# Two-layer graph attention with residual layernorms: the sums of x1 emitted right behind its transposes, and the opening's exponentials and weight sums in other places

## The chip, the core and the metric

The kernel runs on one core of a Trainium2 chip, as one launch. The metric is device time in microseconds (us); the median of three runs is taken. Times in the profile count from the first instruction of one profiled execution.

## The reference

The input x holds 128 graphs of 64 nodes with 768 features, so 8192 tokens; `adj` is a 64x64 mask for each graph. Two layers follow one another, each `layernorm(x + gnn(x))`, all in fp32.

Layer 0 is a gated graph attention with 12 heads of 64 features:

```
h    = x @ W                           # per head
attn = src(tanh(h)) + dst(tanh(h))^T   # src, dst: dot products with w_src, w_dst
attn = leaky_relu(attn, 0.2); attn = where(adj, attn, -999); p = softmax(attn)
f    = elu(p @ h + b);  gate = sigmoid(x @ H_w.T + H_b)
x1   = layernorm(x + gate * f + (1 - gate) * x)
```

Layer 1 is dense attention with 6 heads of 128 features inside each graph:

```
q, k, v = x1 @ Wq, x1 @ Wk, x1 @ Wv
out = layernorm(x1 + softmax(q k^T / sqrt(128), masked) v @ Wf + bf)
```

## The kernel before, in words

**Tiles.** A tile is 128 tokens (two graphs), a pair `p` is two tiles, `t0 = 2p` and `t1 = 2p + 1`. There are 32 pairs. The first half of the span (to about 1490 us) does layer 0 for every pair and the product for `v` of layer 1. The second half does q, k, attention and the output of layer 1; the change does not touch it.

**Products.** A 256x768x768 product is done by a Strassen scheme on 2x2 blocks: seven block products of three matmuls each, instead of eight. Class `Job` holds one such product: "h" (x @ W), "g" (the gate) and "v" (x1 @ Wv). Block product number i of job h is written h1 to h7. Products 3, 5, 6 and 7 need sums of the input's blocks, s4, s1, s2 and s3 (`block_sums`, L240 to L243); products 4 to 7 read sums of weight blocks (`weight_sums`, L216 to L219; product 4 reads T4, 5 reads T1, 6 reads T2, 7 reads T3, made at L218, L216, L217 and L219). For h and g the input sums are `sx`, made by GpSimd (POOL) from x. For v they are `sv`, made by VectorE (DVE) from `x1T`, the transposed x1.

Several products of a job accumulate in the same bank of PSUM: y takes 1, 6, 7, 4 one on top of the other, and between them the partial sum has to be read out ("way out": `S.copy` on ScalarE, ACT, for h and v; an addition on DVE for the gate). So h6 waits for the way out of h1, h7 for that of h6, h4 for that of h7.

**Order.** Everything is emitted in the order of the program, and each engine works through its own list in that order. A turn of the loop over `p` runs a list of products (FIRST for p = 0, SECOND for p = 1, then TURN); after product number `pos` of the list, the previous product's way out is emitted, then the other steps that have been put at `pos`. The steps belong to the new pair p (`at(pos, new, ...)`) or to the old pair q = p - 1 (`was(pos, ...)`); the tables FIRST_AT, SECOND_AT, SECOND_OLD, THIRD_AT and LAST_AT shift a position in the first, second, third and last turn. A position past the end of a list is carried into the next turn: with 13 products in FIRST, position 16 of turn 0 is position 3 of turn 1.

**Steps of a tile.** `products` (tanh of h on ACT, a multiplication on DVE, L889, and one on POOL, L890), `terms` (a reduction to `sd` on DVE, L897, a store to DRAM, `dstd`, and two loads that spread it, `dd`), `with_bias` (POOL, L913, and two loads `hx`), `logits` (DVE, L926, needs dd), `leaky` (ACT, L936), `masked` (three DVE operations, L942 to L949), `exps` (ACT, L955, writes `prob`). In the next turn: `probs_by_nodes` (TensorE, PE, transposes prob into PSUM bank `pTp`, ACT copies it to `pT`), `attend` (PE, `av`), `features` (DVE reads av, L1003 and L1004; ACT exp, L1011), `gate_tanh` (ACT, L1067 and L1068), `residual` (POOL, L1017), `elu1`, `gated`, `stats`, `normed` (layernorm: DVE, POOL, ACT), `by_features` (PE transposes x1 into `x1Tp`, ACT copies it to `x1T`), then `v_begins`, which sets up the sums `v_sums` and the job v, the four sums, and `spill_features`, a store of x1T. SyncE (SP) issues all transfers from one list.

In the regular turn `by_features(t0)` stands at 11, `v_begins` at 12, `products(n0)` at 12, `terms(n1)` at 13, v1 and v2 are products 14 and 15, g4 is 16, v6, the first to need a sum of x1 (s2), is 17.

During turns 2 to 30 POOL also makes sums of the weights for the second half (`sum_weights`, L366).

Of the kernel before, what the change touches and what calls it, by code (L numbers as in the profile page):

```python
# [52 lines left out]

FIRST = ["h1", "h2", "h5", "h6", "g1", "h7", "g2", "h4", "g6", "g5", "g7", "h3", "g3"]

FIRST_AT = {3: 0, 6: 10, 8: 3, 11: 8, 12: 12, 13: 12, 14: 13, 15: 14, 16: 14, 17: 14, 18: 15, 19: 16, 20: 17}
SECOND = [
    "h1", "G4", "h2", "g1", "g2", "h6", "h5", "h7", "g6", "h4",
    "g5", "g7", "h3", "g4", "g3", "H1", "v1", "v2", "v6", "v5", "v7", "H2",
]  # L60
SECOND_AT = {11: 10, 12: 13, 13: 13, 14: 14, 15: 14, 16: 15, 17: 16, 18: 18, 19: 19, 20: 20}
SECOND_OLD = {
    7.5: 12, 0: 7, 1: 7, 2: 8, 3: 9, 4: 10, 5: 11, 6: 12, 7: 12, 8: 13, 9: 14, 11: 15, 12: 15, 15: 16, 16: 17, 19: 19,
}


# [29 lines left out]
    + [f"q{n}" for n in (0, 1, 2, 3, 4, 5, 6, 8, 7, 9, 10, 11, 12)]  # L96
    + ["v1", "v2", "v6", "q13", "v5", "v7", "q14", "v4", "v3"]
)
LAST_AT = {7.5: 8, 3: 3, 4: 4, 5: 5, 6: 6, 7: 7, 8: 9, 9: 10, 11: 12, 12: 13, 15: 15, 16: 17, 19: 18}


PARTS = ("v", "sp", "sc", "ex", "mult", "split", "send", "turn", "join", "cp", "ctx")
# [24 lines left out]
TURNS = {  # L127
    0: (FIRST, FIRST_AT, {}),
    1: (SECOND, SECOND_AT, SECOND_OLD),
# [5 lines left out]
def kernel(  # L135
# [34 lines left out]
    V, S, G, T = nc.vector, nc.scalar, nc.gpsimd, nc.tensor  # L170
# [30 lines left out]
    def load_weight(src, tag, name, order=(B11, B21, B22, T3)):  # L201

        w = wpool.tile([P, 7, HK, HALF], F32, tag=tag, name=name)
        for block in order:
            load_block(src, w, block)
        return w
# [6 lines left out]
    def weight_sums(eng, w):  # L213

        return [
            lambda: eng.tensor_tensor(w[:, T1], w[:, T3], w[:, B11], ALU.subtract),  # L216
            lambda: eng.tensor_tensor(w[:, T2], w[:, B22], w[:, T1], ALU.subtract),  # L217
            lambda: eng.tensor_tensor(w[:, T4], w[:, B21], w[:, T2], ALU.subtract),  # L218
            lambda: eng.tensor_tensor(w[:, T3], w[:, B22], w[:, T3], ALU.subtract),  # L219
        ]  # L220
# [535 lines left out]
    with ExitStack() as ph, ExitStack() as ph_r:  # L756
# [43 lines left out]
        hw_w = weights["k"] = load_weight(hwT, "wb", "hw_wk", (B11, B21, T3, B22))  # L800
# [5 lines left out]
        t1, t2, t4, t3 = weight_sums(V, w0_w)  # L806
        all_of((t1, t2, t3, t4))
        wv_w = wpool.tile([P, 7, HK, HALF], F32, tag="wc", name="wv")
# [30 lines left out]
        def h_job(p):  # L839
            def at(m, n):  # L840
                return h_of(p, m)[:, n * J0 : (n + 1) * J0, :E0]

            def as_heads(b):
                return b.rearrange("p (j e) -> p j e", e=E0)

            return token_job(
                f"h{p}",
                A[p],
                w0_w,
                lambda mn, b: S.copy(at(*mn), as_heads(b)),  # L850
                lambda mn, b: V.tensor_tensor(at(*mn), as_heads(b), at(*mn), ALU.add),
                lambda b: S.copy(at(1, 0), as_heads(b)),
            )

        def gate_job(p):
            def at(m, n):
                return gate_of(p, m)[:, n * HALF : (n + 1) * HALF]

            def bias(n):
                return hb_bc[:, n * HALF : (n + 1) * HALF]  # L860

            return token_job(
                f"g{p}",
                A[p],
                hw_w,
                lambda mn, b: V.tensor_tensor(at(*mn), b, bias(mn[1]), ALU.add),
                lambda mn, b: V.tensor_tensor(at(*mn), b, at(*mn), ALU.add),
                lambda b: V.tensor_tensor(at(1, 0), b, bias(0), ALU.add),
            )
# [213 lines left out]
        def value_sums(q):  # L1083
            B[q], v_sums[q] = sums_of(V, sb, "sv", x1Ts[q], f"v{q}")
# [21 lines left out]
        v_sums, carried = {}, {}  # L1106
        summing = sum_weights(sb)
        for p in range(NP + 1):
            q = p - 1
            new, old = p < NP, 0 <= q < NP  # L1110
            t0, t1, n0, n1 = 2 * q, 2 * q + 1, 2 * p, 2 * p + 1
            if new:
                jobs["G"] = jobs.get("g")
                jobs["h"], jobs["g"] = jobs["H"] if p == 2 else h_job(p), gate_job(p)
            plan = {}

            turn, of_new, of_old = TURNS.get(p, (TURN, {}, {})) if new else (LAST, {}, LAST_AT)

            def at(pos, ok, *acts, places=of_new):
                if ok:  # L1120
                    plan.setdefault(places.get(pos, int(pos)), []).extend(acts)

            def was(pos, *acts):
                at(pos, old, *acts, places=of_old)

            def do(f, *args):
                return lambda: f(*args)

            def v_begins():
                value_sums(q)  # L1130
                jobs["v"] = v_job(q)


            was(0, do(probs_by_nodes, t1))
            at(0, old, do(exps, t0), do(gate_tanh, t1), places={0: 6} if p == 1 else of_old)
            was(1, do(residual, t1))
            was(2, do(attend, t1), do(gate_tanh, t0))
            was(3, do(features, t1), do(probs_by_nodes, t0), do(residual, t0))
            was(4, do(elu1, t1), do(gated, t1))
            was(5, do(attend, t0), do(stats, t1))  # L1140
            was(6, do(features, t0), do(normed, t1))
            was(7, do(elu1, t0))
            was(7.5, do(gated, t0))
            was(8, do(by_features, t1), do(stats, t0))
            was(9, do(normed, t0))
            was(12, do(v_begins))
            was(15, lambda: v_sums[q][0](), lambda: v_sums[q][1](), do(spill_features, q))
            was(16, lambda: v_sums[q][2]())
            was(19, lambda: v_sums[q][3]())

            at(0, p + 1 < NP, do(load_xT, p + 1))
            at(3, new, lambda: adjs.__setitem__(p, load_adj(sb, 2 * p, PAIR, f"adj_{p}")))
            at(6, new, do(mask, p))
            at(4, 0 <= p - 2 < NP, do(spill_values, p - 2))
            at(8, new, do(inputs, p))
            at(11, new, do(products, n1))
            was(11, do(by_features, t0))
            at(12, new, do(products, n0))
            at(13, new, do(terms, n1), do(with_bias, n1))
            at(14, new, do(terms, n0), do(with_bias, n0))  # L1160
            at(15, new, do(plus_one, p))
            at(16, new, do(logits, n1))
            at(17, new, do(leaky, n1))
            at(17, p + 1 < NP, do(x_sums, p + 1), places={17: 12} if p == 0 else of_new)
            at(18, new, do(masked, n1), do(logits, n0))
            at(19, new, do(exps, n1), do(leaky, n0))
            at(20, new, do(masked, n0))

            if p == NP - 1:

                at(2, True, do(load_wide, "q", wq, range(4)))
                at(8, True, do(load_wide, "q", wq, range(4, 8)))
                at(12, True, do(load_wide, "q", wq, range(8, NW)))
                at(9, True, do(load_wide, "k", wk, range(4)))
                at(15, True, do(load_wide, "k", wk, range(4, 8)))
                at(18, True, queries_begin)
                at(20, True, do(load_wide, "k", wk, range(8, NW)), lambda: jobs["rows"].ready(2))
            if p == NP:
                flush()
                for act in plan.pop(0):  # L1180
                    act()
            if p == 0:
                for pos, act in zip((6, 7, 8, 9), weight_sums(V, hw_w)):
                    at(pos, True, act, places={})
                for block in (B11, B21, T3, B22):
                    at(8, True, do(load_block, wv, wv_w, block))
                at(7, True, lambda: V.tensor_scalar(b01_bc, b01_bc, 1.0, None, ALU.add))
            if p == 1:
                at(14, True, third_begins, places={})
                for pos, act in zip((4, 5, 7, 8), weight_sums(V, wv_w)):  # L1190
                    at(pos, True, act, places={})
            for pos, acts in carried.items():
                plan[pos] = acts + plan.get(pos, [])
            carried = {pos - len(turn): acts for pos, acts in plan.items() if pos >= len(turn)}
            for pos, item in enumerate(turn):
                step(jobs[item[0]], int(item[1:]))
                for act in plan.get(pos, ()):
                    act()
                if 2 <= p < NP - 1:
                    for _ in range(1 + pos % 2):  # L1200
                        next(summing, None)
                if item[0] == "q":
                    jobs["rows"].ready(int(item[1:]) + 4)
            if p == NP - 2:
                drain(summing)
            if old:
                jobs["u"] = jobs["v"]
# [4 lines left out]
    with ExitStack() as ph:  # L1212
# [45 lines left out]
        for g in range(1, NG):  # L1258
# [26 lines left out]
            p = 2 * g - 2  # L1285
# [7 lines left out]
        p = 2 * NG - 2  # L1293
# [66 lines left out]
```

## Time and profile before

| | |
|---|---|
| median of 3 runs | 2900.05 us (2900.02 to 2900.45) |
| the profiled execution, whole | 2898.46 us |
| its span, first to last instruction | 2896.7 us |
| PE busy | 2844.1 us (98%) |
| DVE busy | 1936.7 us (67%) |
| POOL busy | 1289.3 us (45%) |
| ACT busy | 1061.6 us (37%) |
| mean granted PE clock | 0.997 |

The table says how long each engine was busy in the span. A line of the timeline gives the start, the duration, the engine, the source line, the operation, what it writes and reads, the shapes, how many instructions were merged, and in square brackets how long the engine was idle before it and what it waited for. A block product of three matmuls counts six there[...].

### The profile page before, as it was taken

The page shows a single profiled execution, that of the slowest core. Times are in us where ns is not written, and L with a number is a line of the kernel's source. Part 1 is how long each engine was busy: PE and PEld are TensorE (multiplying, and loading weights), DVE is VectorE, ACT ScalarE, POOL GpSimd, SP SyncE. Part 2 cuts the span into 40 slices and gives each one's busy share as a digit, 9 for nine tenths or more (in the row PEclk, how much of TensorE's full clock was granted, in tenths as well). Part 3 has the DMA queues.
Part 4 walks back from the last instruction along what each step waited for, and adds up shares of the span by engine and source line. Part 5 has one row for each costly group of instructions (what it writes and reads, how often), then busy time and mean ns, then how long its engine had stood idle before and what let it go on. Part 6 is the DMA issues. An engine that isn't in the chain of part 4 may idle for free.

```text
span 2896.7 us, 47873 instructions
## 1 busy us (share of the span) xinstructions
PE 2844.1 (98%) x18252; PEld 2074.9 (72%) x18252; DVE 1936.7 (67%) x3203; ACT 1061.6 (37%) x1896; POOL 1289.3 (45%) x1253
## 2 busy tenths in 40 slices
PE   7899999999999999999999999999999999999998
PEld 4566556665566655666668888888888888888886
DVE  6888788888878888887874545555545555554556
ACT  2444444444444444444443123333213333322332
POOL 2434454444535444333443454444545443444534
PEclk9999999999999999999999999999999999999999
DMA  5344444544444444333353434432324333223332
GB/s 176 116 154 154 149 136 150 159 142 149 144 154 147 141 141 139 120 122 104 119 203 83 124 101 110 107 91 75 86 82 111 110 101 93 70 84 95 110 88 74
DMA packets 322068, 348.73 MB, mean 120 GB/s; under 512 B 147888, under 2 KB 247216, under 8 KB 321840
## 3 DMA queue, kind: packets, MB, share of 16 engines
q1 hardware_dynamic: 321840, 345.66, 39.1%
q8 instruction: 146, 2.39, 0.4%
q14 instruction: 82, 0.67, 0.1%
HBM read 198.48 MB, written 122.29 MB: 111 GB/s over the span
## 4 chain that ended last, share of the span: by engine, by line
PE 84%; DVE 8%; DMA 3%; ACT 2%; issue 1%; POOL 1%; SPq 1%; POOLq 0%; DVEq 0%; ACTq 0%
PE z_o L494 8%; PE z_k L447 8%; PE z_q L447 8%; PE y_h L270 7%; PE y_v L270 6%; PE y_g L270 6%; PE y_k L447 6%; PE y_o L494 6%; PE y_q L447 5%; PE z_h L270 4%; PE z_v L270 3%; PE z_g L270 3%; PE x_g L270 2%; PE sp L550 2%; PE cp L634 2%; PE x_h L270 2%
## 5 line engine op out<-in xcount | busy, mean ns | idle before, releaser
L574 ACT ACTIVATE sc<-sc 128x512 f32<-128x512 f32 x48 | 30.7, 639 | 615.0 <-DVE sc L571 615.0
L695 POOL TENSOR_TENSOR y<-y,bf_bc 128x768 f32<-128x768 f32 x64 | 114.7, 1815 | 288.3 <-DMA y<-x1d 288.3
L507 DVE TENSOR_TENSOR y<-y,z_o 128x256 f32<-128x256 f32 x320 | 127.5, 418 | 139.6 <-PE z_o L494 139.4
L494 PE MATMUL z_o<-wf,so 128*128 128x256 f32 x896 | 215.8, 383 | 2.3 <-DVE y L507 1.2
L447 PE MATMUL z_q<-xs,w_wq 128*128 128x256 f32 x896 | 213.5, 381 | 0.3 <-POOL xs L411 0.3
L411 POOL TENSOR_TENSOR so<-ctxT 128x256 f32<-128x256 f32 x224 | 160.1, 731 | 92.3 <-PE y_o L494 47.0
L447 PE MATMUL z_k<-xs,hw_wk 128*128 128x256 f32 x840 | 198.5, 379 | 0.0
L1017 POOL TENSOR_TENSOR x<-gate,x 128x768 f32<-128x768 f32 x64 | 118.2, 1848 | 159.6 <-ACT gate L1068 145.3
L494 PEld LDWEIGHTS z_o<-wf,so 128*128 128x128 f32 x896 | 167.2, 190 | 26.9 <-issue 2.0
L447 PEld LDWEIGHTS z_q<-xs,w_wq 128*128 128x128 f32 x896 | 168.7, 190 | 24.3 <-POOL xs L411 0.7
L322 POOL TENSOR_TENSOR rs_b<-ve_b,minus_half 128x1 f32<-128x1 f32 x64 | 40.5, 632 | 312.9 <-DVE ve_b L320 312.1
L890 POOL TENSOR_TENSOR th<-th,wsd 128x768 f32<-128x768 f32 x64 | 117.3, 1832 | 139.8 <-DVE th L889 139.8
L447 PEld LDWEIGHTS z_k<-xs,hw_wk 128*128 128x128 f32 x840 | 159.5, 190 | 21.7
L322 POOL TENSOR_TENSOR rs_a<-ve_a,minus_half 128x1 f32<-128x1 f32 x64 | 36.0, 562 | 307.8 <-DVE ve_a L320 307.8
L411 POOL TENSOR_TENSOR xs<-r,r 128x512 f32<-128x512 f32 x112 | 147.7, 1336 | 39.3 <-DMA r<-x1Td 22.1
L462 DVE TENSOR_TENSOR qT<-qT,z_q 128x512 f32<-128x512 f32 x96 | 66.0, 688 | 141.7 <-PE z_q L447 141.7
L270 PE MATMUL y_v<-wv,sv_v 128*128 128x384 f32 x384 | 136.4, 491 | 9.3 <-DVE sv_v L241 7.5
L270 PE MATMUL y_h<-w_wq,xT 128*128 128x384 f32 x384 | 136.5, 492 | 8.7 <-DMA w_wq<-in_w_dram 8.1
L462 DVE TENSOR_TENSOR kT<-kT,z_k 128x512 f32<-128x512 f32 x96 | 66.1, 688 | 112.3 <-PE z_k L447 111.2
L270 PE MATMUL y_h<-w_wq,sx_x 128*128 128x384 f32 x384 | 136.5, 492 | 4.2 <-ACT h L850 4.2
L270 PE MATMUL y_g<-hw_wk,sx_x 128*128 128x384 f32 x384 | 136.2, 491 | 2.5 <-DVE hw_wk L219 2.2
L270 PE MATMUL z_v<-wv,sv_v 128*128 128x384 f32 x384 | 137.5, 494 | 1.0 <-DVE v L880 1.0
(165 smaller groups left out, 6913.3 us busy)
## 6 DMA issues: line engine op xcount, KB each, us to landing
x<-in_x_dram SPq DMA_DIRECT2D x64, 384.0 KB, 3.6
dd<-dstd SPq DMA_DIRECT2D x128, 192.0 KB, 3.4
x1d<-x SPq DMA_DIRECT2D x64, 384.0 KB, 2.6
x1Td<-x1T SPq DMA_DIRECT2D x32, 768.0 KB, 4.3
vd<-v SPq DMA_DIRECT2D x64, 384.0 KB, 3.1
r<-x1Td SPq DMA_DIRECT2D x96, 256.0 KB, 3.5
v<-vd SPq DMA_DIRECT2D x384, 64.0 KB, 2.3
y<-x1d SPq DMA_DIRECT2D x64, 384.0 KB, 5.4
```

What stands on the lines that cost most here:

```text
L270: T.matmul(to[:, : self.n], lhsT, rhs, start=kc == 0 and not more, stop=kc == HK - 1, skip_group_check=more,)
L322: G.tensor_tensor(rstd, ve, minus_half, ALU.pow)
L411: G.tensor_tensor(t, self.of(x[0]), self.of(x[2]), x[1])
L447: T.matmul(b[:, half * W2 : (half + 1) * W2], w[:, kc, half * P : (half + 1) * P], x[:, kc, :], start=half == kc == 0 and not more, stop=k ...
L462: V.tensor_tensor(at, at, b.rearrange("p (h t) -> p h t", h=2), ALU.add if sign > 0 else ALU.subtract,)
L494: T.matmul(b[:, :W2], x[:, kc, :], w[:, kc, :], start=kc == 0 and not more, stop=kc == 1, skip_group_check=more,)
L507: V.tensor_tensor(at, at, self.banks[path][:, :W2], ALU.add if sign > 0 else ALU.subtract)
L550: T.matmul(self.sp_[gr * N : (gr + 1) * N, (i * 2 + a) * N : (i * 2 + a + 1) * N], qT[:, 2 * self.f + a, at], kT[:, 2 * self.f + a, at], s ...
L634: T.matmul(self.cp_[a][e, at], self.v_[rows, i, gr, e], self.scT_[rows, at], start=True, stop=True,)
L695: G.tensor_tensor(y, y, pools["bf"], ALU.add)
L890: G.tensor_tensor(th[:, 1, :], th[:, 1, :], wsd[:, 1, :], ALU.mult)
L1017: G.tensor_tensor(xp, st[t]["gate"], xp, ALU.mult)
```

## The change

It moves instructions and adds none.

1. `v_begins` now stands after `by_features(t0)` in the text, and emits the first sum of x1 (s1) with it at position 12; the second (s2) goes to 13. Both stood at 15. SECOND_OLD and LAST_AT get an entry for 13. `spill_features` stays at 15, the sums s3 and s4 at 16 and 19.
2. In turn 0, the weight sums of the gate: T3 is emitted at 8 and T4 at 9, where T4 was at 8 and T3 at 9.
3. In turn 1, the weight sums of v: T1, T2 and T4 all at 0, where they stood at 4, 5 and 7. T3 stays at 8.
4. For pair 0: `exps(1)`, `leaky(0)` and `masked(0)` from positions 3, 3 and 4 of turn 1 to 6; `exps(0)` and `gate_tanh(1)` from 6 to 8; `residual(1)` from 7 to 8.

```diff
-FIRST_AT = {3: 0, 6: 10, 8: 3, 11: 8, 12: 12, 13: 12, 14: 13, 15: 14, 16: 14, 17: 14, 18: 15, 19: 16, 20: 17}
+FIRST_AT = {3: 0, 6: 10, 8: 3, 11: 8, 12: 12, 13: 12, 14: 13, 15: 14, 16: 14, 17: 14, 18: 15, 19: 19, 20: 19}
 SECOND_OLD = {
-    7.5: 12, 0: 7, 1: 7, 2: 8, 3: 9, 4: 10, 5: 11, 6: 12, 7: 12, 8: 13, 9: 14, 11: 15, 12: 15, 15: 16, 16: 17, 19: 19,
+    7.5: 12, 0: 7, 1: 8, 2: 8, 3: 9, 4: 10, 5: 11, 6: 12, 7: 12, 8: 13, 9: 14, 11: 15, 12: 15, 13: 15, 15: 16, 16: 17, 19: 19,
 }
-LAST_AT = {7.5: 8, 3: 3, 4: 4, 5: 5, 6: 6, 7: 7, 8: 9, 9: 10, 11: 12, 12: 13, 15: 15, 16: 17, 19: 18}
+LAST_AT = {7.5: 8, 3: 3, 4: 4, 5: 5, 6: 6, 7: 7, 8: 9, 9: 10, 11: 12, 12: 13, 13: 14, 15: 15, 16: 17, 19: 18}
...
-            at(0, old, do(exps, t0), do(gate_tanh, t1), places={0: 6} if p == 1 else of_old)
+            at(0, old, do(exps, t0), do(gate_tanh, t1), places={0: 8} if p == 1 else of_old)
...
-            was(12, do(v_begins))
-            was(15, lambda: v_sums[q][0](), lambda: v_sums[q][1](), do(spill_features, q))
+            was(15, do(spill_features, q))
...
             was(11, do(by_features, t0))
+
+            was(12, do(v_begins), lambda: v_sums[q][0]())
+            was(13, lambda: v_sums[q][1]())
             at(12, new, do(products, n0))
...
             if p == 0:
-                for pos, act in zip((6, 7, 8, 9), weight_sums(V, hw_w)):
+                h1, h2, h4, h3 = weight_sums(V, hw_w)
+                for pos, act in zip((6, 7, 8, 9), (h1, h2, h3, h4)):
                     at(pos, True, act, places={})
...
             if p == 1:
                 at(14, True, third_begins, places={})
-                for pos, act in zip((4, 5, 7, 8), weight_sums(V, wv_w)):
+                for pos, act in zip((0, 0, 0, 8), weight_sums(V, wv_w)):
                     at(pos, True, act, places={})
```

Compared engine by engine, the lists of PE and SP are the same in both programs. The list of DVE differs in every turn of the first half; those of ACT and POOL differ in turn 1 alone.

## The prediction

> **What bounds the kernel now.** I read the page first, then PE's waits, then the timelines of the opening and of one regular turn. PE is busy for nearly the whole span, and the change neither adds nor reorders a PE instruction, so only PE's waits, and the slow matmuls behind them, can move the time.
>
> ```profile
> PE 2844.1 (98%) x18252; PEld 2074.9 (72%) x18252; DVE 1936.7 (67%) x3203; ACT 1061.6 (37%) x1896; POOL 1289.3 (45%) x1253
> ```
>
> PE's waits, by who ended them:
>
> ```profile
> PE y_h L270 <- DMA w_wq<-in_w_dram: 8.1, 1, 8.1
> PE y_v L270 <- DVE sv_v L241: 7.5, 9, 1.4
> PE y_h L270 <- ACT h L850: 4.8, 2, 4.2
> PE x1Tp L966 <- ACT x L327: 4.5, 2, 3.3
> ...
> PE y_g L270 <- DVE hw_wk L219: 2.2, 1, 2.2
> ```
>
> The first is the load at the start and stays. The second is v6 waiting for s2, in nine turns (0.62 us in turn 1, 6.9 in later ones, 7.0 with a wait of 0.12 too short for the list). The rest lies in turns 0 and 1. PE's timeline there, g7, h3 and g3 of pair 0, then h5 and h7 of pair 1:
>
> ```profile
> 33.03 3.39 PE L270 MATMUL y_g<-hw_wk,sx_x 128*128 128x384 f32 x6 [2.16 <-DVE hw_wk L219]
> 36.22 2.65 PE L270 MATMUL z_h<-w_wq,sx_x 128*128 128x384 f32 x6
> 38.70 2.10 PE L270 MATMUL z_g<-hw_wk,sx_x 128*128 128x384 f32 x6
> ...
> 52.24 2.10 PE L270 MATMUL z_h<-w_wq,sx_x 128*128 128x384 f32 x6
> 58.52 4.18 PE L270 MATMUL y_h<-w_wq,sx_x 128*128 128x384 f32 x6 [4.18 <-ACT h L850]
> ```
>
> A product costs 2.10 us, and 1.94 from start to start; behind a wait over 2 us it is slower. DVE in the same stretch, T4 and T3 of the gate, the second reduction to sd and the first logits:
>
> ```profile
> 28.74 1.35 DVE L218 TENSOR_TENSOR hw_wk<-hw_wk 128x1152 f32<-128x1152 f32 x1
> ...
> 30.48 2.50 DVE L219 TENSOR_TENSOR hw_wk<-hw_wk 128x1152 f32<-128x1152 f32 x1
> ...
> 43.37 1.75 DVE L897 TENSOR_REDUCE sd<-th 128x24 f32<-128x1536 f32 x1
> 48.99 2.75 DVE L926 TENSOR_TENSOR att<-dd,sd 128x768 f32<-128x768 f32 x1 [3.88 <-DMA dd<-dstd]
> ```
>
> g7 waits for L219. DVE then sits 3.88 us for dd, and from 48.99 on it is almost never idle until features(1) at 71.49. A regular turn on DVE:
>
> ```profile
> 1236.28 0.55 DVE L851 TENSOR_TENSOR h<-z_h,h 128x384 f32<-128x384 f32 x1
> 1237.91 1.17 DVE L889 TENSOR_TENSOR th<-th,wsd 128x768 f32<-128x768 f32 x1 [1.08 <-ACT th L888]
> 1239.00 1.74 DVE L897 TENSOR_REDUCE sd<-th 128x24 f32<-128x1536 f32 x1
> ...
> 1243.37 1.31 DVE L240 TENSOR_TENSOR sv_v<-x1T 128x384 f32<-128x384 f32 x1
> 1244.71 1.23 DVE L241 TENSOR_TENSOR sv_v<-sv_v,x1T 128x384 f32<-128x384 f32 x1
> ```
>
> s1 and s2 come after two reductions, though x1T was complete at 1237.13 (ACT's copies).
>
> **What the Trainium skill says.** "SBUF — State Buffer", "Who interferes with whom": a VectorE tensor_tensor with both inputs in SBUF and a GpSimd operation that reads SBUF lock each other out for a whole instruction; tensor_reduce never contends. The trace agrees: L926 took 2.75 us while POOL ran L913, 1.50 without; L897 took 1.75 beside a POOL multiplication. "TensorE: Matmul & The Clock Gate", "Part 1: The HAM clock gate", says that activity releases a throttle on PE's clock. The trace agrees in kind: behind 2.16 us of waiting the product took 3.39 us, behind 1.4 us 2.17.
>
> **Part 2, T3 ahead of T4.** T3 takes T4's slot at 28.74 and ends at 30.1; PE wants g7 at 30.87. The wait of 2.16 goes, and with it the slow stretch: g7 to h3 takes 3.19, h3 to g3 2.48, against 1.94 each, so 1.79. Together 3.95 us. T4 now runs until 33.0 and is wanted by G4 at about 38.5. One addition (L866) stands between the two in both orders.
>
> **Part 3, three weight sums of v.** 3 x 1.27 us (start to start) leave DVE's full stretch after 49 and fill its wait for dd. Their blocks had landed by 34.25 and the sums come after both reductions, so dd isn't delayed. But POOL then runs L890, L913, the four sx and L913, 41.4 to 50.4. In alternation each sum waits for a POOL operation of about 1.0. With everything 4.0 earlier, the reductions end at 41.1; the sums run 41.8-43.1, 44.05-45.3, 46.3-47.6, with sx in between; logits(1) starts behind the fourth sx, 48.6 to 50.1. Shifted alone it would have been 45 to 47.7. So the fight costs 2.4 of the 4.0. POOL's sx come in time: s2 at 44.05 for h6 at 46.2, s3 at 46.3 for h7 at 50.
>
> **Part 4, exponentials.** Now h7 waits 4.18 since the way out of h6 stands on ACT behind exps(1) and leaky(0). It moves ahead of both, and only leaky(1) remains in front, to 51.0. So h7 starts at 51.5 (PE ready at 50.05), not 54.5. Next late is prob(1): masked(1) ends at 54.05 on DVE, exps(1) at 54.95, so the transposes wait until 55.0 (ready 53.4). g6 waits for the addition L866 until 56.55. Attend follows at 58.5, and through POOL's memset the way out of h7, at 60.1; exps(0), which now stands behind it, ends at 60.95, when its input is ready anyway. features(1) ends at 63.8 (before 71.49, 7.7 earlier). gate_tanh(0) and residual(0) follow late: POOL's L1017 (1.82) then locks out elu1 at 64.5 to 66.3, which costs 1.3. The tile's x1 comes at 69.1 instead of 75.45: 6.4 us earlier. This chain (DVE, ACT, layernorm) ends PE's waits before the x1 transposes, so PE gains the same. No transfer is reissued elsewhere: SP's list is unchanged, and its stores simply come earlier.
>
> The opening thus gives 6.4, plus 0.6 as s2 now stands ahead of the logits, 7.0. Without the fight for the port, logits(1) is 3.7 earlier and the sum is about 11. Were Part 4 to bring nothing, Part 2 alone gives 4.0.
>
> **Part 1, s1 and s2.** Regular turn: s1 may start at 1237.2, in the idle time before L889, but POOL's L890 (1236.44 to 1238.26) locks it out; it ends at 1238.8. L889 ends at 1239.7 (before 1239.08), s2 at 1240.2. v6 wants s2 at 1246: its wait goes in every turn, 7.0 us. Behind s1 and s2 now queue both reductions. The first ends at 1241.9 instead of 1240.74: dstd, dd and logits come 1.2 later. In this turn dd landed at 1246.43 and was read at 1247.14, so logits lose 0.5. exps(1) ended at 1254.30, and PE's transposes began 1.55 later: hidden, with 1.05 left. The gate's additions (L866) slip 1.2, to 1242.4, and g4 reads them at 1244.14. In turns with L366 on POOL the delay may be 2.0, and a turn whose 1.4 us wait goes has that much less slack: in the turn at 693 us I find 0.86 slack against 0.7 to 1.4 of delay. I take 1.0 off for such turns: 6.0 of 7.0 kept (bounds 3.0 and 7.5). In turn 31 dd comes late (4.63 idle) behind weight loads that land until 1473, so the 1.2 mostly disappears there; 0.2 lost, at most 1.2.
>
> **Sum.** -7.0 -6.0 +0.2 = -12.8 us. The profiled execution took 2898.46 (span 2896.7 and 1.76 around it) and becomes 2885.7; it ran 1.6 below the median of 2900.05. Taken off the median: 2887.2 us.
>
> **Rivals.**
> (a) The opening without the fight: -11.4 -6.5, 2882. For it: PE and POOL drift, and nothing forces alternation. Against: POOL is busy throughout, and L926 did take 2.75 there.
> (b) Half the gain: the later dd hands back 3 to 4 us in the turns that waited, and the opening gives only Part 2's 4.0 and a little: -5 to -9, 2891 to 2894.5. For it: the slack of 0.86 above.
> (c) No difference: the opening's wait for one late thing is replaced by the next, as PE is early to everything there, and the turns hand back theirs; under 5.8 us. Against: Part 2 has no cover, its 4.0 alone almost reach the bound.
> (d) Slower: dd. Logits have 0.55 to 1.5 us between landing and reading, then 1.55 to the transposes, so about 2.1 in each turn. A delay of 2.8 would cost 0.7 in each of 30 turns, 21 us, and the sum becomes +7: 2907. It decides from 2.5 on (12 us, gain gone). For it: POOL operations of 1.82 and 0.74 can hit s1 and s2 both. Against: where they fell thickest I find 2.0, and much of a delay is idle time in front of L889 already.
>
> **How the numbers follow.** Main case 0.60 (2883.5 to 2891), (a) 0.13, (b) 0.13, (c) 0.08, (d) 0.06. A measurement here can tell 0.2%, 5.8 us, so faster means below 2894.25: 0.86; same 0.08; slower 0.06. Leaving out (c), (d) and a little of (a) gives 2881 to 2894.5.
>
> **What would show it.** Right: no wait at L219 near 33 us; h7's wait under 2 us and the transposes' near 1.5; x1's first transposes 6 us earlier; no wait on sv_v. DVE's L926 idle for dd in regular turns, exps(1) to transposes between 0.5 and 1.5. Wrong: new waits of PE on prob (L955) in regular turns, L240 waiting for ACT's x1T while an addition for PE stands behind it, or logits(1) in turn 1 later than 51.

## The result, and the profile after

The changed kernel takes 2906.47 us (median of 16 runs, 2903.34 to 2911.84), the kernel before 2899.88 in the runs beside it (16 runs, 2895.39 to 2902.71): a ratio of 1.0024, 95% interval 1.0017 to 1.0031. It is slower by about 6.6 us, where 12.8 less were predicted. The profiled execution took 2906.8 us, with a span of 2905.0: 8.3 us over the span of before.

I cut the two spans where PE starts the transposes of tile t0's x1, once in each turn (turn 2 is the loop's p = 2, which transposes the x1 of pair 1), to see where the time went:

| stretch | before | after | difference |
|---|---|---|---|
| start to turn 2's transposes (opening) | 130.34 | 122.67 | -7.67 |
| from there to turn 31's (29 turns) | 1333.50 | 1349.05 | +15.55 |
| the rest | 1432.86 | 1433.28 | +0.42 |
| span | 2896.7 | 2905.0 | +8.3 |

The opening brought what was predicted (7.0). The 29 turns, which should have given back 6 us, took 15.55 more. The page's totals hardly show it, but the page's chain of work that ended last does:

```profile
PE 2847.0 (98%) x18252; PEld 2074.5 (71%) x18252; DVE 1930.1 (66%) x3203; ACT 1057.8 (36%) x1896; POOL 1299.6 (45%) x1253
...
PE 63%; DVE 17%; DMA 6%; ACT 5%; issue 5%; POOL 2%; SPq 1%; POOLq 0%; DVEq 0%; ACTq 0%
```

Before, this chain was PE 84%, DVE 8%, DMA 3% and ACT 2%. PE is busy for the same 98%, but the work that sets the end now runs for more than a third of the span over other engines. PE's waits in the changed kernel, by who ended them (total us, times, longest):

```profile
PE pTp L966 <- DVE rden L1003: 14.1, 15, 1.6
...
PE pTp L966 <- DVE fo L1004: 4.7, 27, 0.2
...
PE pTp L966 <- ACT prob L955: 2.8, 2, 1.5
...
PE y_h L270 <- ACT h L850: 1.1, 2, 0.7
```

The waits for `sv_v` (7.5), for h7 (4.8 together with h4's) and for L219 (2.2) have gone or shrunk, as intended. In their place stands a wait that nobody had named: the transposes of the second prob wait for features(1), L1003 and L1004, which read the attention's result and so free the bank that these transposes write. Before, the same two rows had 1.7 and 1.1 us.

**The opening.** PE's timeline of the changed kernel, g7 and h3, then h7 and the first transposes of prob:

```profile
30.78 2.12 PE L270 MATMUL y_g<-hw_wk,sx_x 128*128 128x384 f32 x6
32.73 2.10 PE L270 MATMUL z_h<-w_wq,sx_x 128*128 128x384 f32 x6
...
50.70 2.17 PE L270 MATMUL y_h<-w_wq,sx_x 128*128 128x384 f32 x6 [0.39 <-ACT h L850]
54.27 0.87 PE L966 MATMUL pTp<-ident,prob 128*128 128x128 f32 x6 [1.39 <-ACT prob L955]
```

g7 waits for nothing and no slow stretch follows it. h7 waits 0.39 us instead of 4.18. DVE of the changed kernel in that stretch, three weight sums of v and the first logits:

```profile
41.00 2.02 DVE L216 TENSOR_TENSOR wv<-wv 128x1152 f32<-128x1152 f32 x1
43.05 2.04 DVE L217 TENSOR_TENSOR wv<-wv 128x1152 f32<-128x1152 f32 x1
45.12 2.04 DVE L218 TENSOR_TENSOR wv<-wv 128x1152 f32<-128x1152 f32 x1
47.08 2.23 DVE L926 TENSOR_TENSOR att<-dd,sd 128x768 f32<-128x768 f32 x1
```

Two of POOL's four `sx` sums in the same stretch:

```profile
41.88 1.99 POOL L241 TENSOR_TENSOR sx_x<-sx_x,xT 128x384 f32<-128x384 f32 x1
43.83 2.11 POOL L242 TENSOR_TENSOR sx_x<-xT 128x384 f32<-128x384 f32 x1
```

DVE's sums take 2.0 us each where they took 1.27 from start to start without company, and the three `sx` sums beside them 1.99 to 2.11 us, where the first one took 1.00: the two engines go in turn. The logits start at 47.08 and end at 49.31; the prediction had 48.6 and 50.1.

**A regular turn.** DVE of the changed kernel in the turn that answers to the one shown of before, the turn with x1's transposes at 1242.32:

```profile
1243.32 1.93 DVE L240 TENSOR_TENSOR sv_v<-x1T 128x384 f32<-128x384 f32 x1
1245.17 0.94 DVE L889 TENSOR_TENSOR th<-th,wsd 128x768 f32<-128x768 f32 x1
1246.04 0.54 DVE L241 TENSOR_TENSOR sv_v<-sv_v,x1T 128x384 f32<-128x384 f32 x1
1246.51 1.74 DVE L897 TENSOR_REDUCE sd<-th 128x24 f32<-128x1536 f32 x1
...
1254.76 1.52 DVE L926 TENSOR_TENSOR att<-dd,sd 128x768 f32<-128x768 f32 x1 [2.77 <-DMA dd<-dstd]
```

s1 (L240) takes 1.93 us for 0.55 us of work, since POOL's L890 has started just before it:

```profile
1243.01 1.82 POOL L890 TENSOR_TENSOR th<-th,wsd 128x768 f32<-128x768 f32 x1 [4.26 <-DVE th L889]
```

The reduction to `sd` comes about a microsecond later than it did, measured against PE, and with it the store and the loads of `dd`. s1 and s2 used to fill DVE's wait for `dd`; now DVE stands idle there. Its idle time for `dd` between 130 and 1460 us (total, times, longest), first in the kernel before, then in the changed one:

```profile
DVE att L926 <- DMA dd<-dstd: 2.9, 6, 0.9
DVE att L926 <- DMA dd<-dstd: 56.9, 32, 3.0
```

What the two kernels' times hang on is plainest in the chain that ended last, taken over this one turn. First the changed kernel (start, us, what; the pieces in between are ACT's and DVE's own steps):

```profile
1238.61 1.95 PE y_h L270 x6
...
1243.40 1.85 DVE sv_v L240
...
1246.12 0.47 DVE sv_v L241
1246.58 1.67 DVE sd L897
...
1250.24 4.43 DMA dd<-dstd
...
1270.00 0.57 DVE fo L1004
...
1270.70 0.52 PE pTp L966 x3
```

And the kernel before, the end of the same stretch:

```profile
1261.39 2.13 PE z_v L270 x6
1263.53 0.80 PE pTp L966 x6
```

Before, every piece of the turn's chain is PE's. After, the chain leaves PE behind the last product of h's y (1240.56) and comes back only at the transposes (1270.70), 30.1 us later, through tanh, s1, s2, the reduction, the store and loads of `dd`, both logits, the second exponential, ACT's gate operations, L851 and features(1). s1 and s2 are in it: they are no longer fill but part of the way.

The windows of these 29 turns (start and end, length, PE busy) split the 15.55:

```profile
122.67:1471.72 1349.05, 1328.96 (x7136) 803.81 (x7135) 1079.61 (x1567) 579.17 (x929) 598.23 (x536) 1.00 0.43 139
```

PE's busy time is 1324.62 before, so of the 15.55 us 11.2 are more idle time and 4.3 longer PE rows. The longer rows are mostly transposes that hold a wait; one is a product that took 3.79 us instead of 2.10 behind a wait.

### The profile page after: what moved, and what is told of

Same layout as the page of the kernel before. It is cut to its first block, busy times and chain, and to the rows that moved or that the text cites. A ratio compares the mean times of both kernels' runs of the same rounds, so it can differ in the third digit from the quotient of the medians.

```text
span 2905.0 us, 47846 instructions
## 1 busy us (share of the span) xinstructions
PE 2847.0 (98%) x18252; PEld 2074.5 (71%) x18252; DVE 1930.1 (66%) x3203; ACT 1057.8 (36%) x1896; POOL 1299.6 (45%) x1253
## 4 chain that ended last, share of the span: by engine, by line
PE 63%; DVE 17%; DMA 6%; ACT 5%; issue 5%; POOL 2%; SPq 1%; POOLq 0%; DVEq 0%; ACTq 0%
PE z_o L494 8%; PE z_k L447 8%; PE z_q L447 8%; PE y_k L447 6%; PE y_o L494 6%; PE y_q L447 6%; PE y_h L270 5%; PE y_g L270 3%; DMA dd<-dstd 3%; DVE att L926 3%; PE z_h L270 2%; PE sp L550 2%; PE cp L634 2%; DMA dstd<-sd 2%; DVE att L942 2%
## 5 line engine op out<-in xcount | busy, mean ns | idle before, releaser
L890 POOL TENSOR_TENSOR th<-th,wsd 128x768 f32<-128x768 f32 x64 | 125.8, 1967 | 149.7 <-DVE th L889 146.1
L926 DVE TENSOR_TENSOR att<-dd,sd 128x768 f32<-128x768 f32 x64 | 108.7, 1699 | 62.6 <-DMA dd<-dstd 62.5
L270 PE MATMUL y_v<-wv,x1T 128*128 128x384 f32 x384 | 138.2, 497 | 1.1 <-ACT v L879 0.9
L270 PE MATMUL z_h<-w_wq,sx_x 128*128 128x384 f32 x384 | 137.5, 494 | 0.0
```

Of the source, the lines that this page charges most:

```text
L270: T.matmul(to[:, : self.n], lhsT, rhs, start=kc == 0 and not more, stop=kc == HK - 1, skip_group_check=more,)
L890: G.tensor_tensor(th[:, 1, :], th[:, 1, :], wsd[:, 1, :], ALU.mult)
L926: V.tensor_tensor(att3, dd.rearrange("p (m a) -> p a m", a=H0), sd[:, H0:].unsqueeze(2).to_broadcast([P, H0, N]), ALU.add,)
```

## The experiments

The theory that I took to the chip (A): the work of a turn that runs from the new pair's tanh over `dd`, the logits and the exponentials to features(1) is already as long as PE's own turn. So every delay ahead of the logits lengthens the turn. Rivals: (B) the opening's rearrangement spoils the later turns; (C) nothing new is late, and PE merely waits elsewhere for what the earlier s2 gave it. The prediction's own view was that the turns have about 2 us to spare between the logits and the transposes; then something else would have to cost, such as the port that DVE shares with POOL or a slow PE. Runs of the kernel before gave 2901.62 us (33 runs) beside the first four experiments and 2902.24 (10 runs) beside the others. Quiet turns are the last seven of the 29, from turn 24's transposes on: POOL's weight sums (L366) are over by then, the last one at 1126 us before and 1132 after. A quiet turn takes 45.62 us before, 45.83 to 45.97 after.

### The opening alone

Against the changed kernel:

```diff
-            was(15, do(spill_features, q))
+            was(15, lambda: v_sums[q][0](), lambda: v_sums[q][1](), do(spill_features, q))
-            was(12, do(v_begins), lambda: v_sums[q][0]())
-            was(13, lambda: v_sums[q][1]())
+            was(12, do(v_begins))
```

> The change without its part 1: the sums s1 and s2 stay where they were, all edits of the opening are in. Theory A (the early sums delay the first reduction and with it the round trip of sd through DRAM; features(1) then frees its PSUM bank later and PE waits at the transposes of the second prob): the opening's 7.5 us are gained and nothing is lost later, 2892.5 us, no wait of PE on DVE L1003 above 0.5 us. Rival B (the new opening puts all later turns into a worse rhythm, the sums are harmless): 2905 or more. Rival C (nothing new is late; PE merely waits elsewhere for what the early s2 gave it): 2892.5 as under A.

It took 2895.47 us (13 runs), a ratio of 0.998 (0.9972 to 0.9989): 6.1 us faster. Quiet turns take 45.61, as before, and PE's wait of before is back:

```profile
PE y_v L270 <- DVE sv_v L241: 7.8, 10, 1.6
```

So the opening's part is worth about what was predicted for it (the result is 3.0 above the 2892.5 expected here), the later turns don't suffer from it, and (B) falls.

### The sums of x1 alone

Against the kernel before:

```diff
-            was(12, do(v_begins))
-            was(15, lambda: v_sums[q][0](), lambda: v_sums[q][1](), do(spill_features, q))
+            was(15, do(spill_features, q))
...
+            was(12, do(v_begins), lambda: v_sums[q][0]())
+            was(13, lambda: v_sums[q][1]())
```

(and the entries for 13 in the two tables).

> Part 1 alone: s1 and s2 at 12 and 13, the opening as before. A: turns 2 to 29 lose the same 15.5 us as in the changed kernel, the opening gains only the 0.6 of s2: 2914 to 2915 us, waits of PE on L1003 and L1004 near 19 us. B: no loss, 2893 to 2900. C: within 1 us of before, 2899 to 2901.

2912.16 us (5 runs), 1.0039 (1.0025 to 1.0053): 10.5 us slower. The profiled execution was its longest, 2919.95, so its trace is read for kinds of waits alone: 18.1 us on L1003 and 4.6 on L1004, none on `sv_v`. The two halves add up to +4.4 us, against +6.6 measured for the whole: near enough for their intervals, and the loss is all in this half. (C), which gave 2899 to 2901, falls too.

### The sums behind the second tile's additions

s1 and s2 stand between the two reductions, so `dd` of the first logits isn't delayed:

```diff
-            was(12, do(v_begins), lambda: v_sums[q][0]())
-            was(13, lambda: v_sums[q][1]())
+            was(12, do(v_begins))
+            at(14, old, lambda: v_sums[q][0](), lambda: v_sums[q][1](), places={14: 15} if p == 1 else of_old)
```

> The change with s1 and s2 between the two reductions: behind the first reduction and the two additions of the gate, ahead of the second reduction. The first sd then leaves DVE as early as in the kernel before, and s2 still comes ahead of v6. A: the loss of 15.5 goes, first reduction to transposes of the first prob back at 15.1 us; v6 waits no more, but the transposes of the second prob stood within 0.4 us of their bank in the kernel before, so most of the 7.0 comes back as a wait there: 2890 to 2893 us. My prediction's view (the 7.0 is gained whole once the delay is gone): 2886. B: 2905 or more.

2903.59 us (13 runs), 1.0007 (0.9999 to 1.0015): better than the change, but 11 us above the range that A gave. DVE hardly waits for `dd` any more (0.2 us in all between 130 and 1460). Yet the quiet turn is 45.95, like the changed kernel's. DVE of this kernel in such a turn:

```profile
1242.81 1.92 DVE L241 TENSOR_TENSOR sv_v<-sv_v,x1T 128x384 f32<-128x384 f32 x1
...
1247.96 1.51 DVE L926 TENSOR_TENSOR att<-dd,sd 128x768 f32<-128x768 f32 x1
```

The sums now meet POOL's other operation, L913, and s2 takes 1.92 us. The logits end 13.98 us after the start of x1's transposes (1235.49); before it was 13.63, in the changed kernel 13.96. So the delay of `dd` as such isn't what counts: in these three kernels the quiet turn is longer where the first logits end later, whatever makes them late.

### The gate's tanh of the second tile one product later

The other end of the same way: ACT runs the way out of h1 ahead of one tile's two gate operations (L1067, L1068), so features(1) comes earlier.

```diff
-            at(0, old, do(exps, t0), do(gate_tanh, t1), places={0: 8} if p == 1 else of_old)
-            was(1, do(residual, t1))
+            at(0, old, do(exps, t0), *[do(gate_tanh, t1)] * (p == 1), places={0: 8} if p == 1 else of_old)
+            was(1, *[do(gate_tanh, t1)] * (p != 1), do(residual, t1))
```

> The whole change, and in the regular turns gate_tanh(t1) with its residual stands one product later, so that ACT copies h (the way out of h1) ahead of the two gate operations; DVE's addition L851, which stands ahead of features(1), waited 2.47 us for that copy. A: the chain from dd to features(1) is some 1.7 us shorter, waits of PE on L1003 shrink from 14.1 to 3 us or less: 2885 to 2892 us, the early reads of dd (DVE idle 1 to 3 us a turn) unchanged. If the bank that features(1) frees is not what PE waits for: 2905 to 2907. B: 2905 or more.

2907.06 us (13 runs), 1.0019 (1.0011 to 1.0027): no gain over the change, where A gave 2885 to 2892. The waits on L1003 have gone from the list and those on L1004 are down to 2.1 us, but PE's longest wait is now:

```profile
PE x1Tp L966 <- ACT x L327: 17.0, 19, 3.3
```

features(1) is earlier, but ACT's exponential for it (L1011) still starts behind both tiles' gate operations, at 1270.57 against 1270.59 in the same turn of the changed kernel, whose turns are timed almost alike up to here. So elu and the layernorm are as late as they were, and the way meets PE at the next place, x1's transposes. It isn't one wait that has to be removed: the whole way round is too long. That the time came out as if features(1) didn't matter hides one thing: in the seven quiet turns the shorter way did help, 319.1 us together against 321.1 in the changed kernel and 319.3 before. The new waits at x1's transposes all lie in turns ahead of these.

### One more microsecond at the old place

To test the slack of "about 2.1 in each turn" of rival (d) by itself, s1 is emitted twice at its old place, in the kernel with the opening alone:

```diff
-            was(15, lambda: v_sums[q][0](), lambda: v_sums[q][1](), do(spill_features, q))
+            was(15, *[lambda: v_sums[q][0]()] * 2, lambda: v_sums[q][1](), do(spill_features, q))
```

> The opening alone (run e1_opening) with s1 made twice at its old place, in turns 1 to 32: 0.5 to 0.6 us of DVE more in each turn, 1.0 where POOL holds the port. Theory A, as it now stands (the round of a pair from the transposes of x1 through reduction, dd, logits, exps, features and layernorm back to PE is as long as PE's own turn, so what is added on it is added to every turn): turns of 45.6 us become 46.1 to 46.6, 14 to 25 us over the 2895.5 of e1_opening, so 2910 to 2920. My prediction's view (about 2.1 us of slack between logits and transposes in each turn): 2896 to 2898.

2919.77 us (5 runs), 1.0054 (1.0042 to 1.0067), over 20 us more than the opening alone. In a quiet turn the two s1 take 2.58 us together (one took 1.31), and the turn is 46.74 instead of 45.61: 1.27 us of work cost 1.13. PE's waits:

```profile
PE y_v L270 <- DVE sv_v L241: 29.4, 30, 2.6
```

In a quiet turn, v6 and the second transposes of prob:

```profile
1257.18 2.17 PE L270 MATMUL y_v<-wv,sv_v 128*128 128x384 f32 x6 [1.11 <-DVE sv_v L241]
...
1274.45 0.82 PE L966 MATMUL pTp<-ident,prob 128*128 128x128 f32 x6
```

The time lies in A's range, but not for A's reason. s2 comes 1.27 us later, and v6 waits 1.11 us for it: that wait alone is nearly the whole 1.13. At the second transposes PE, late by now, waits for nothing (0.82 us is their row without a wait). So the run shows that s2 had no slack ahead of v6 at its old place. The slack between the logits and the transposes, which it was meant to test, it leaves open; that rests on the changed kernel and on the experiments before and after this one.

### The changed kernel without the wait for dd

```diff
-                dd.rearrange("p (m a) -> p a m", a=H0),
+                wsd[:, 0, :].rearrange("p (m a) -> p a m", a=H0),
```

> The whole change, but the logits read a resident row (wsd) where they read dd; the store and the loads of dd are still issued, nothing waits for them but the next user of their buffer. So the logits don't hold the destination terms: left out of the computation. A: DVE no longer sits 1 to 3 us for dd in a turn, the quiet turns fall from 45.9 to PE's own 45.4, all waits on L1003 and L1004 go: 2906.5 less some 32, 2872 to 2880 us. If the lateness came from DVE's own work or the port alone and dd didn't matter: 2900 to 2907.

2878.47 us (5 runs), 0.992 (0.9906 to 0.9933). s1 still takes 1.93 us behind L890, but the quiet turn is 45.38 to 45.39. DVE of this kernel at features(1):

```profile
1240.42 0.20 DVE L1003 RECIPROCAL rden<-av 128x6 f32<-128x6 f32 x1 [0.37 <-PE av L987]
```

features now waits for PE, where in both kernels it follows L851 without a wait, its own way late. With this way shortened PE sets the turn, and 45.38 is PE's own pace. So the kernel before, with 45.62, was 0.24 us per turn above it: the two were almost equal, and there was no slack to spend. And since s1's 1.93 us are still there and the loss isn't, the time on the port doesn't cost by itself, only by what it makes late.

### s1 in the idle time ahead of the tanh

The changed kernel with s1 moved ahead of `products(n1)`, where DVE idles 2.5 us for ACT's tanh, and s2 back at its old place:

```diff
+            at(11, old, do(v_begins), lambda: v_sums[q][0](), places={11: 15} if p == 1 else of_old)
             at(11, new, do(products, n1))
-            was(12, do(v_begins), lambda: v_sums[q][0]())
-            was(13, lambda: v_sums[q][1]())
...
-            was(15, do(spill_features, q))
+            was(15, lambda: v_sums[q][1](), do(spill_features, q))
```

> The change with s1 at 11 ahead of products(n1), where DVE sat 2.5 us for ACT's tanh and POOL was idle (s1 reads tile t1 alone, transposed since position 8), and s2 back at 15. A: s1 leaves the round and costs nothing, neither reduction nor dd is delayed, logits(1) end about 0.7 earlier than in the kernel before, v6 no longer waits: quiet turns 45.4, 2883 to 2890 us, faster than the opening alone. If the early place of s1 by itself were the harm: 2900 or more.

2885.3 us (5 runs, 2883.95 to 2887.48), 0.9941 (0.9929 to 0.9954): faster than both kernels. DVE:

```profile
1219.90 0.55 DVE L240 TENSOR_TENSOR sv_v<-x1T 128x384 f32<-128x384 f32 x1
1222.75 0.96 DVE L889 TENSOR_TENSOR th<-th,wsd 128x768 f32<-128x768 f32 x1 [2.30 <-ACT th L888]
```

s1 runs free of POOL in 0.55 us, and DVE still idles 2.30 us behind it: it costs nothing. The logits end 12.35 us after x1's transposes (1223.10) instead of 13.63, features waits 0.36 us for PE, and the quiet turn is PE's 45.38. PE's waits of 14.1 and 4.7 us for features have shrunk to 3.4 and 2.1, and the wait of 7.5 on `sv_v` to 0.4. The 29 turns take 1326.42 us. This is what part 1 was expected to do, and more.

### The same, with s2 where the change has it

```diff
+            at(11, old, do(v_begins), lambda: v_sums[q][0](), places={11: 15} if p == 1 else of_old)
             at(11, new, do(products, n1))
-            was(12, do(v_begins), lambda: v_sums[q][0]())
             was(13, lambda: v_sums[q][1]())
```

> As e7_s1_early, but s2 at 13 as in the change: of the change's part 1 only s1's place differs, so only its 1.93 us behind POOL's L890 is taken away. A: the first reduction is 0.5 us later than in the kernel before instead of 1.0 to 2.0, logits start as dd lands and meet less of POOL: quiet turns 45.4 to 45.6, 2884 to 2893 us. If s2 ahead of the reduction is the harm rather than s1 behind the port's lock: 2900 to 2906.

2893.78 us (6 runs), 0.9969 (0.9958 to 0.9981), 0.8 above the expected range. Each kernel taken against the kernel before in its own runs (1.0024 for the change, 0.9969 here), s1's place alone is worth about 16 us, and s2's another 8.5 by the medians. s2 ahead of the first reduction takes 0.55 us in a quiet turn, and the logits end 13.40 us after x1's transposes instead of 12.35: DVE waits for `dd` again (48.9 us in all between 130 and 1460, 18.0 with s2 behind the reductions), and the waits for L1003 are 8.2 us instead of 3.4.

## Why the prediction was wrong

**Part 2, T3 ahead of T4: right.** The wait for L219 and the slow products behind it have gone: g3 starts at 34.67 instead of 38.70, 4.03 us earlier (3.95 predicted). T4 ran from 30.56 to 33.06, as the prediction had it.

**Part 3, the weight sums: right, its cost put a little high.** The sums alternate with POOL's, and the second reduction ended at 41.08 (41.1 predicted), the logits at 49.31 (50.1). Against the 47.7 without the fight, it cost 1.6 us instead of 2.4.

**Part 4, the exponentials: right, a little too low.** h7 waited 0.39 us (predicted: ready 50.05, start 51.5), the transposes 1.39 (1.6), the product g6 0.55 (0.9). What the prediction calls x1 at 69.1 instead of 75.45 is the end of L1029, the sum ahead of the layernorm: it came at 68.34. x1's first transposes started at 74.95 instead of 82.12, 7.2 us earlier (6.4 predicted). Up to turn 2's transposes 7.67 us are saved where 7.0 were predicted, and the opening alone measures 6.1 us (3.2 to 8.1 by its interval).

**Part 1, s1 and s2: wrong, in the step "hidden, with 1.05 left".** The delay was about as predicted: 1.2 us for the first reduction, about 1.0 in the trace. From the end of the reduction to the first prob's transposes there were 15.10 us before (1240.74 to 1255.84) and 14.09 after (1248.24 to 1262.33). The slack left between exps(1) and these transposes was as predicted too: 1.13 us (1261.20 to 1262.33), 1.05 predicted. "Logits lose 0.5" was near as well: they end 13.96 us after x1's transposes instead of 13.63. What failed is where the slack was read. I followed the lateness to one consumer, the first prob's transposes, found 1.55 us there between exps(1) and PE, and stopped. But the same way goes on: logits(0), exps(0), the gate operations, the way out of h1, L851, features(1). All of these stand in DVE's or ACT's order behind the first logits, and there the second prob's transposes wait. That place had no slack: its waits on L1003 and L1004 grew from 0.7 and 0.9 us to 14.1 and 4.5 in these 29 turns. Three things on the traces of before say so, and I read past them:

- the list of PE's waits had these transposes on L1003 (1.7 us) and L1004 (1.1), 0.7 and 0.9 of it in these 29 turns, where the prediction says that all but v6's wait lies in turns 0 and 1;
- features(1) followed L851 without idle time of DVE, so it wasn't PE that it waited for;
- the row of the second transposes took 0.97 us, the first one's 0.82 (1263.36 and 1255.84), though both are six identical instructions.

DVE and PE of the kernel before in that turn:

```profile
1255.84 0.82 PE L966 MATMUL pTp<-ident,prob 128*128 128x128 f32 x6
...
1261.72 0.56 DVE L851 TENSOR_TENSOR h<-x_h,h 128x384 f32<-128x384 f32 x1 [2.47 <-ACT h L850]
1262.19 0.19 DVE L1003 RECIPROCAL rden<-av 128x6 f32<-128x6 f32 x1
...
1263.36 0.97 PE L966 MATMUL pTp<-ident,prob 128*128 128x128 f32 x6
```

With PE's pace now known, the last point can be read: the row of six merged instructions holds a wait in its middle. In the experiments where features(1) comes early the same row takes 0.82 us.

**"Its wait goes in every turn, 7.0": the wait went, the gain didn't.** v6 waited for s2 in eight of the 29 turns, 6.9 us. Turn against turn, four of these eight got shorter, by 0.76 to 1.40 us, so there the gain came. The other four got longer, by 0.82 to 1.53: in them PE now waited 0.75 to 1.61 us at the second transposes, a few products on, so the wait at v6 had covered lateness that was there anyway or was new. Together the eight lost 0.5 us: of "6.0 of 7.0 kept" nothing was left. The other 21 turns, which had no wait to give back, lost 15.1: +0.33 us in the quiet turn shown, more in turns with POOL's L366 (one takes 49.50 us instead of 45.62), with 1.7 us in that one for a slow product behind a wait. Sum -6.0 predicted, +15.55 measured.

**Rival (d)** named the right place, logits late behind s1 and s2 (by `dd` or, as the third experiment showed, without it), and a time that was close (2907), but got there with a delay of 2.8 us and said that it "decides from 2.5 on". So its time was close by luck. In the quiet turn shown, logits that end 0.33 us later go with a turn that is 0.33 us longer: it decides from about nothing on. Its "2.1 in each turn" was built from two gaps, one of them the slack at the first transposes.

**The port.** The prediction counted POOL's L890 against s1 and was right about its size (an end at 1238.8 for a start near 1237; the trace has 1.93 us). It wasn't taken for a reason to look for a place outside L890's reach. Such a place existed some 4 us earlier, in DVE's own idle time: s1 at 3.2 us ahead of x1's transposes of tile t0 instead of 1.0 behind their start. The prediction let s1 start at 1237.2, when all of x1T was complete, but s1 reads tile t1 alone, whose half was copied by 1230.7. There s1 costs 0.55 us and the turn falls to PE's pace.

What stays open is what makes the turns with POOL's weight sums so much dearer. The seven quiet turns lost 1.75 us together, 0.25 each, with only 0.17 of a wait on L1004 in each; the 22 turns ahead of them lost the other 13.8. All 15 waits on L1003 lie there (the last one at 1086 us). POOL's L366 stands at different instructions in each of these turns; that it makes the delay larger is likely, but I haven't taken them apart.

## What to carry to other kernels

When a step is delayed, follow its result to every later consumer on the bounding engine, not to the first; what the delayed engines do next in their own order, down to the buffer that they free a stage later, belongs to the way. A bounding engine at 98% doesn't mean that the other way round the loop has slack: the chain of one turn, and whether the last stage of that way waits for the bounding engine or the other way about, tell how close the two are. A wait that disappears is a gain only if no other wait a few instructions on covers the same lateness, and work moved earlier should go into idle time that ends later than the work does, and outside the stretch in which another engine holds the port.

## What the runs showed of the hardware

- s1, placed just behind the start of POOL's multiplication L890 (1.82 us), took 1.93 us (the median of 29 turns) instead of 0.55. The Trainium skill's "SBUF — State Buffer", "Who interferes with whom", says that the shared port is an exclusive lock; here DVE lost 1.38 us to it, and s1 ended 0.42 us behind POOL's operation.
- With both engines' operations back to back in the opening, the two alternated: 2.02, 2.04 and 2.04 us for DVE's weight sums against 1.99, 2.11 and 2.11 for POOL's sums, in turn.
- A wait of 1.61 us, and 0.18 more between the two halves of the transposes, was followed by a product of 3.79 us instead of 2.10 in one turn. PE's timeline of the changed kernel:

```profile
432.59 0.52 PE L966 MATMUL pTp<-ident,prob 128*128 128x128 f32 x3 [1.61 <-DVE rden L1003]
...
433.64 3.79 PE L270 MATMUL y_h<-w_wq,sx_x 128*128 128x384 f32 x6
```

All products of this group together (h6 and h7 of 29 turns) take only 1.7 us more than before (123.5 us of busy time, 121.8 before), which is this one. Yet PE waited there in 15 turns, twice more for the same 1.61 us (at 713.98 and 1086.34) with a product of 2.10 behind. The clock that PE was granted tells them apart: 0.51 from 433.60 to 435.60 us, behind the first wait, and 1.00 from 713.90 to 718.00 and from 1086.20 to 1091.00. In the kernel before it was 0.64 from 33.00 to 36.20, where g7 took 3.39 us. So a wait's full price isn't fixed by its length alone, and the prediction's "over 2 us" is no limit: a slow product can follow 1.61 us, and needn't.
